# Four copies of an expert's first half, chosen by a jump per expert

## The chip, the cores and the metric

The kernel runs on one core of one Trainium2 chip. The metric is the device time of one execution in microseconds (us). Before the change it is 5404.11 us, the median of three runs from 5396.59 to 5407.47 us. Smaller is better.

A core has engines that run side by side, each with its own queue of instructions that it works through in order: TensorE (PE, matrix products and transposes), VectorE (DVE), ScalarE (ACT), GpSimd (POOL) and SyncE (SP, which here only starts transfers). They wait for each other by semaphores. A tile framework writes the waits; it also plans the order of each engine's queue by simulated times, and it may move an instruction ahead of others of the same straight stretch of code where its inputs are ready.

## The reference

One decoder layer in float32 on 8 sequences of 512 tokens of width 512 (N = 4096 tokens): a state-space block, a cross attention, and a mixture of experts, each followed by a layer norm. The change lies in the mixture of experts, and this is its core:

```python
E, K, CAP_FACTOR = 32, 4, 1.25
cap = max(1, int(CAP_FACTOR * N * K / E))          # 640 slots for each expert
w, idx = _gate(xf, wg)                             # 4 experts and weights for each token
oh = jax.nn.one_hot(idx.reshape(-1), E, dtype=jnp.int32)
pos = (jnp.cumsum(oh, axis=0) * oh).sum(-1) - 1    # place in the expert's queue
keep = pos < cap                                   # later tokens are dropped
...
xe = xp[buf_tok].reshape(E, cap, DIM)              # an empty slot holds zeros
h = silu(einsum('ecd,edh->ech', xe, w1)) * einsum('ecd,edh->ech', xe, w3)
out = einsum('ech,ehd->ecd', h, w2) * buf_w.reshape(E, cap, 1)
y = zeros((N + 1, DIM)).at[buf_tok].add(out)[:N]
z = silu(xf @ sw1) * (xf @ sw3) @ sw2              # the shared expert
return y + z
```

Every expert has 640 slots. How many of them hold a token depends on the data; 4096 x 4 / 32 = 512 is the mean. The slots are filled from the first on.

## The kernel before

`layers` does the first two blocks, the gate and the shared expert. For each token and chosen expert it computes a slot (`locate`; `taken[:, j, :]` counts the tokens of each expert so far, and after the last sequence `taken[:, SC, :]` holds the total of each expert) and scatters the token's row, with its weights and its own number behind it, into `xbuf` in DRAM (`send`). Slots that no token takes keep a row of zeros with the number of a spare row. `based` in DRAM holds the input of the last norm, to which the experts' outputs are added.

`experts` is the stage of the change. An expert has 640 slots, as five tiles of 128 (CJ = 5). For each expert e:

- `load(e)` starts four transfers on SyncE's queue: `xe` (640 rows, 1.36 MB, L1250) and the weights `w1`, `w3`, `w2` (1 MB each, L1253). Each has two buffers, so that one for expert e + 2 waits until expert e has finished with its own. For `xe` the last user is the last scatter of expert e, which reads the row numbers in it.
- `flip(j)` turns slot tile j by four transposes on TensorE (L1285) and an eviction on VectorE (L1286) into `xT`, with the model width on the partitions and the slots along the free dimension.
- `hidden(r)`, for r = 0 and 1, is the first half: `silu(x w1) * (x w3)`, written to `hT`. Each product is done by a scheme of seven block products in the place of eight (Strassen's, in Winograd's form): both operands are split in two by two blocks, and VectorE prepares sums of blocks (`sums_w`, L1276; `sums_x`, L1293 to L1296; `sums_w2`, L1308). The slots are split into two halves of HALF = 320 columns, slots 0 to 319 and 320 to 639. A block product is two matmul calls (L1314), each of which shows as two instructions in the profile; 2 x 2 x 7 x 2 x 2 = 112 instructions of 320 columns for each expert. ScalarE copies partial results out of PSUM (L1328) and applies silu (L1341), VectorE adds and multiplies (L1335, L1339).
- `give` is the second half: `hT w2`, seven block products for slots 0 to 511 (56 instructions of 256 columns), and a plain product for the fifth slot tile, slots 512 to 639 (L1416: four matmul calls, eight instructions of 512 columns). Outputs are scaled by the slot's weight (L1387, L1391, L1417, L1444), and `put(j)` on GpSimd's queue (L1394) adds the 128 rows of a slot tile to `based` by an indirect DMA that accumulates. The framework orders two `put`s, since both write `based`. The program's order of them is 4, 0, 1, 2, 3.

While `give` runs, a generator (`between`) puts the five `flip`s of the next expert between the products, and spreads `sums_x` and the sums of `w3` among them; the sums of `w1` of the next expert and of this one's `w2` go between the products of `hidden`. All 32 experts are written out one after the other, without a branch, so that the planner may also move work across experts.

## Time and profile before

| what | us |
|---|---|
| median of three runs | 5404.11 |
| the profiled execution's own time | 5406.28 |
| its span, first to last instruction | 5404.6 |
| TensorE busy in the span | 4672.4 (86%) |
| VectorE busy in the span | 4235.9 (78%) |
| expert stage, from the first transpose to the end of the last second half | 3794 to 5334 |
| in 3794 to 5334: TensorE busy | 1536.97 of 1540 |
| in 3794 to 5334: VectorE busy | 897.23 of 1540 |
| in 3794 to 5334: ScalarE busy | 426.77 of 1540 |

How to read it: a group row names the line, engine, operation, the tiles as written<-read, their shapes and how often (x); then busy time, the mean of one in ns, and idle time before it with what ended the idle time. A timeline row gives start, duration, engine, line and operation; the ends of matmuls are modelled, so that the distance from start to start is the rate. A windows row gives, for each stretch, its length, busy time of PE, PEld (weight loads), DVE, ACT and POOL with the number of instructions, the TensorE clock that was granted (1.00 is full), the share of the DMA engines' time and GB/s. `SPq` and `POOLq` are queues of those engines; a row of waits names who waited for what, for how long in all, how often, and the longest.

### The profile page before, as it was taken

How to read it: one execution, taken by the hardware profiler on the slowest of the kernel's cores; microseconds unless marked ns; L12 is line 12 of the kernel's file. 1: busy time of each engine (PE TensorE's matmuls, PEld its weight loads, DVE VectorE, ACT ScalarE, POOL GpSimd, SP SyncE). 2: the span in 40 equal slices, each digit the busy share in tenths (PEclk: the TensorE clock that was granted, in tenths of full speed). 3: DMA queues.
4: the chain of work that ended last, by engine and by line, in shares of the span. 5: the costliest groups of instructions: out<-in, count | busy, mean ns of one | idle time of the engine just before them, and what ended most of it. 6: DMA issues, size and time to landing. Idle time of an engine off the chain costs nothing. (4 is left out here: it accounts for less than half of the span.)

```text
span 5404.6 us, 53991 instructions
## 1 busy us (share of the span) xinstructions
PE 4672.4 (86%) x17320; PEld 2476.6 (46%) x17320; DVE 4235.9 (78%) x5369; ACT 2593.6 (48%) x5726; POOL 570.3 (11%) x426
## 2 busy tenths in 40 slices
PE   6768889788888988988888888789999999999994
PEld 3324234234333423433333342333677777777773
DVE  7999899989989989898998998943566555665554
ACT  5566565565656556566565655523222222222223
POOL 1000002002000200200200020011111111111111
PEclk8879989999999999999999999899999999999997
DMA  8875346345444634634544463342344444544544
GB/s 236 266 224 146 87 96 208 81 114 176 114 104 117 197 77 109 189 98 107 174 125 100 117 200 78 91 146 66 103 128 127 123 117 118 127 127 121 129 115 144
DMA packets 486427, 719.03 MB, mean 133 GB/s; under 512 B 117137, under 2 KB 200625, under 8 KB 484096
## 3 DMA queue, kind: packets, MB, share of 16 engines
q1 hardware_dynamic: 450128, 627.16, 41.1%
q0 software_dynamic: 33280, 76.90, 7.5%
q10 hardware_dynamic: 2736, 11.54, 0.5%
q8 instruction: 137, 2.24, 0.2%
q14 instruction: 146, 1.20, 0.1%
HBM read 391.24 MB, written 165.05 MB: 103 GB/s over the span
## 5 line engine op out<-in xcount | busy, mean ns | idle before, releaser
L480 ACT ACTIVATE l_da<-rep,l_aneg 128x256 f32<-128x256 f32 x2048 | 895.0, 501 | 941.8 <-DVE h L501 877.0
L501 DVE TENSOR_TENSOR_SCAN h<-l_da,h 128x1028 f32<-128x1028 f32 x512 | 1166.0, 2292 | 20.3 <-ACT l_da L480 17.7
L494 DVE TENSOR_TENSOR h<-rep,bc 128x1024 f32<-128x1024 f32 x512 | 614.7, 1218 | 103.1 <-PE py L521 84.6
L510 DVE TENSOR_TENSOR h<-h,bc 128x1024 f32<-128x1024 f32 x512 | 619.5, 1217 | 2.1
L521 PE MATMUL py<-h,l_fold 128*32 128x512 f32 x2048 | 368.3, 644 | 113.4 <-DVE h L510 96.5
L813 PE MATMUL ps_s<-l_ka,l_qa 64*128 64x512 f32 x1024 | 325.6, 707 | 137.8 <-DVE mx L815 137.6
L1314 PE MATMUL ps_h<-xT,w 128*128 128x320 f32 x1536 | 435.8, 433 | 0.0
L1394 POOL DMA_INDIRECT based<-y,xe x160 | 255.5, 1597 | 1309.9 <-ACT y L1417 630.0
L1335 DVE TENSOR_TENSOR hT<-ps_h,p 128x320 f32<-128x320 f32 x128 | 62.9, 492 | 378.5 <-PE ps_h L1314 378.5
L815 DVE TENSOR_REDUCE mx<-ps_s 128x2 f32<-128x1024 f32 x256 | 310.2, 1217 | 58.5 <-PE ps_s L813 58.3
L1314 PEld LDWEIGHTS ps_h<-xT,w 128*128 128x128 f32 x1536 | 292.5, 191 | 118.3 <-issue 0.4
L855 PE MATMUL po<-eT,l_va 128*64 128x512 f32 x1024 | 301.5, 670 | 47.6 <-ACT eT L843 43.1
L839 PE MATMUL ps_t<-l_qa,l_ka 64*128 64x512 f32 x1024 | 308.4, 674 | 23.8 <-ACT eT L843 23.1
L843 ACT ACTIVATE eT<-ps_t 128x1024 f32<-128x1024 f32 x256 | 259.0, 1015 | 128.8 <-PE ps_t L839 128.5
L688 POOL DMA_INDIRECT xbuf<-x2t,dest x128 | 217.2, 1697 | 860.4 <-DVE dest L679 760.8
L1314 PE MATMUL ps_h<-t,s 128*128 128x320 f32 x1024 | 286.1, 432 | 0.0
L343 PE MATMUL ps_z<-xnT,wm 128*128 128x256 f32 x1024 | 238.0, 388 | 30.0 <-DVE o L561 24.3
L750 PE MATMUL ps_p<-x2T,wa 128*128 128x512 f32 x512 | 241.5, 626 | 18.1 <-ACT hT L944 10.4
L552 PE MATMUL po<-wm,zs 128*128 128x512 f32 x512 | 244.7, 632 | 13.8 <-DVE z L957 11.9
L343 PE MATMUL ps_x<-xnT,wm 128*128 128x256 f32 x1024 | 246.5, 393 | 4.5 <-ACT xnT L332 2.5
L343 PEld LDWEIGHTS ps_z<-xnT,wm 128*128 128x128 f32 x1024 | 194.6, 193 | 93.0 <-DVE o L561 37.5
L343 PEld LDWEIGHTS ps_x<-xnT,wm 128*128 128x128 f32 x1024 | 196.1, 195 | 80.5 <-issue 43.8
(232 smaller groups left out, 7170.4 us busy)
## 6 DMA issues: line engine op xcount, KB each, us to landing
w<-in_w SPq DMA_DIRECT2D x93, 1024.0 KB
wm<-in_in_proj_w SPq DMA_DIRECT2D x128, 512.0 KB
rep<-dt SPq DMA_DIRECT2D x256, 256.0 KB
rep<-dtx SPq DMA_DIRECT2D x256, 256.0 KB
xbuf<-zero SPq DMA_DIRECT2D x32, 1362.5 KB
xe<-xbuf SPq DMA_DIRECT2D x32, 1362.5 KB
wm<-in_out_proj_w SPq DMA_DIRECT2D x64, 512.0 KB
wa<-in_sw SPq DMA_DIRECT2D x24, 1024.0 KB
```

The lines of the kernel that those rows point to most:

```text
L343: nc.tensor.matmul(ps[:, i, :], w[:, dc, i * P : (i + 1) * P], f["xnT"][:, dc, :], start=(dc == 0), stop=(dc == DC - 1),)
L480: nc.scalar.activation(da[:, n, 1:], dt[:, j, i, :], AF.Exp, scale=aneg[:, 2 * q + i, 2 * jj + j, g : g + 1])
L494: nc.vector.tensor_tensor(h[:, :, 1:], dtx.rearrange("p j i t -> p (j i) t"), f["bc", g][0], ALU.mult)
L501: nc.vector.tensor_tensor_scan(flat, da.rearrange("p n t -> p (n t)"), flat, 0.0, ALU.mult, ALU.add)
L510: nc.vector.tensor_tensor(h[:, :, 0:T], h[:, :, 1:], f["bc", g][1], ALU.mult)
L521: nc.tensor.matmul(f["py"][j * QP : (j + 1) * QP, :, :], fold, hs[j // 2][:, 2 * (j % 2) : 2 * (j % 2) + 2, 0:T], start=False, stop=g == N ...
L813: nc.tensor.matmul(ps[:, j, :], qa[r, lt * P : (lt + 1) * P], ka[r, :], start=True, stop=True)
L815: return lambda: nc.vector.tensor_reduce(mx[:, lt, :].unsqueeze(2), ps, AX.X, ALU.max) and None
L839: nc.tensor.matmul(ps[:, j, :], ka[r, kc * P : (kc + 1) * P], qa[r, :], start=True, stop=True)
L843: nc.scalar.activation(eT, ps, AF.Exp)
L855: nc.tensor.matmul(po[j * 2 * HD : (j + 1) * 2 * HD, :], va[:, kc, i, j * HD : (j + 2) * HD], eT[:, j, :], start=(kc == 0), stop=(kc == SC ...
L1314: nc.tensor.matmul(ps, w[:, n, r * P : (r + 1) * P], x[:, n, :], start=not more and n == 0, stop=n == 1, skip_group_check=more,)
```

## The change

The number of slots that an expert has to compute is chosen at run time from four: 448, 512, 576 and 640, that is 224, 256, 288 or 320 columns of each half.

- After the last sequence's `locate`, three VectorE instructions compute for each expert how many of the limits 448, 512 and 576 its count passes: `arm`, 0 to 3, kept in SBUF in a pool of its own.
- The two halves of the slots are now the even and the odd slots, so that the first `cols` columns of both halves hold slots 0 to 2 cols - 1. `flip` sorts them while it evicts, and `hidden` writes `hT` back in the order of the slots, with a stride of two.
- In the loop over experts, `tc.Switch` with four copies stands around the first half. TensorE, ScalarE and VectorE each read `arm` of the expert into a register, jump to one of the four copies, and jump out to common code after it; GpSimd and SyncE have nothing in the copies. The planner orders the inside of each copy by itself and moves nothing across the jumps.
- A copy zeroes the rest of `hT` where it has fewer than 320 columns, does `hidden` with `cols` columns, then the first two `flip`s of the next expert, and then the fifth slot tile (`fifth`): its product and its eviction where 2 cols > 512, and zeros in its output otherwise. `put(4)` is issued in all cases.
- The other three `flip`s stay in `give`. What the copies write is allocated ahead of them (`room_w`, `room_w2`, `got["y"]`, `nxt["xT"]`).
- For expert e + 1, each of the three engines loads the register in `give` of expert e and gives a hint of the coming jump (`announce`): VectorE behind the sums of `hT`, ScalarE behind the second copy `p1`, TensorE behind the products of the second block. Expert 0 has no hint.
- The PSUM pool of `flip` has two buffers in the place of one, the one of the fifth slot tile one in the place of two.

```diff
+COLS = tuple(range(224, HALF + 1, 32))
...
+        if not clock:
+            many = taken[:, SC, :]
+            more = taken[:, 1, :]
+            nc.vector.tensor_scalar(more, many, float(2 * COLS[0]), None, ALU.is_gt)
+            for c in COLS[1:-1]:
+                to = arm if c == COLS[-2] else more
+                nc.vector.scalar_tensor_tensor(to, many, float(2 * c), more, ALU.is_gt, ALU.add)
...
-    pst = ctx.enter_context(tc.tile_pool(name="e_pst", bufs=1, space=PSUM))
-    pso = ctx.enter_context(tc.tile_pool(name="e_pso", bufs=2, space=PSUM))
+    pst = ctx.enter_context(tc.tile_pool(name="e_pst", bufs=2, space=PSUM))
+    pso = ctx.enter_context(tc.tile_pool(name="e_pso", bufs=1, space=PSUM))
...
     def flip(got, j):
...
-        nc.vector.tensor_copy(got["xT"][:, :, j * P : (j + 1) * P], ps.rearrange("p (c t) -> p c t", c=DC))
+        to = got["xT"].rearrange("p c (k t) -> p c k t", k=2)[:, :, :, j * P // 2 : (j + 1) * P // 2]
+        nc.vector.tensor_copy(to, ps.rearrange("p (c t k) -> p c k t", c=DC, k=2))
...
     def product(ps, w, r, x, more=False):
 
+        cols = ps.shape[-1]
         for n in range(2):
-            nc.tensor.matmul(
-                ps, w[:, n, r * P : (r + 1) * P], x[:, n, :], start=not more and n == 0, stop=n == 1,
+            ins = nc.tensor.matmul(
+                ps, w[:, n, r * P : (r + 1) * P], x[:, n, 0:cols], start=not more and n == 0, stop=n == 1,
                 skip_group_check=more,
             )
-
-    def hidden(got, r, side):
+        return ins
+
+    def hidden(got, r, side, cols):
...
-            to = hT[:, 2 * i + r, k * HALF : (k + 1) * HALF]
+            to = hT.rearrange("p c (t k) -> p c t k", k=2)[:, 2 * i + r, 0:cols, k]
...
-    def give(e, got, side):
+    def fifth(e, got, cols):
+
+        j, y = CJ - 1, got["y"][CJ - 1]
+        if 2 * cols <= j * P:
+            nc.vector.memset(y, 0.0)
+            return
+        po = pso.tile([P, D], F32, tag="po", name="po")
+        for ic in range(DC):
+            nc.tensor.matmul(
+                po, got["hT"][:, ic, j * P : (j + 1) * P], got["w2"][:, ic, :], start=(ic == 0), stop=(ic == DC - 1)
+            )
+        nc.scalar.activation(y, po, AF.Identity, scale=got["x"][:, j, D + e : D + e + 1])
+
+    def give(e, got, side, which):
...
             v = p2.tile([P, HALF], F32, tag=f"{tag}{r}", name=tag)[:, 0:FH]
-            nc.scalar.activation(v, ps, AF.Identity, scale=weight(j))
+            ins = nc.scalar.activation(v, ps, AF.Identity, scale=weight(j))
+            if tag == "p1" and r and e + 1 < E:
+                announce(which, e + 1, ins)
             return v
...
-        for _ in sums_w(got, "hT"):
+        room_w(got, "hT")
+        for ins in sums_w(got, "hT"):
             pass
+        if e + 1 < E:
+            announce(which, e + 1, ins)
...
-        j = CJ - 1
-        po = pso.tile([P, D], F32, tag="po", name="po")
-        for ic in range(DC):
-            nc.tensor.matmul(po, hT[:, ic, j * P : (j + 1) * P], w2[:, ic, :], start=(ic == 0), stop=(ic == DC - 1))
-        nc.scalar.activation(ys[j], po, AF.Identity, scale=weight(j))
-        put(j)
+        put(CJ - 1)
...
+        if e + 1 < E:
+            announce(which, e + 1, ins)
...
     def between(nxt):
 
+        room_w(nxt, "w3")
         sums = sums_w(nxt, "w3")
-        for j in range(CJ):
+        for j in range(2, CJ):
             flip(nxt, j)
             if j == CJ - 1:
                 sums_x(nxt)
             next(sums, None)
             yield
+        for _ in sums:
+            pass
+
+    engines = {mybir.EngineType.PE: nc.tensor, mybir.EngineType.Activation: nc.scalar, mybir.EngineType.DVE: nc.vector}
+
+    def choice(k, e):
+        return engines[k].value_load(arm[0:1, e : e + 1])
+
+    def announce(which, e, ins):
+        k = ins.ins.engine
+        with tc.issue_after(ins.ins):
+            which[k] = choice(k, e)
+            tc.switch_hint({k: which[k]}, len(COLS), label=f"cols{e}")
...
+    which = {k: choice(k, 0) for k in engines}
     for e in range(E):
         got, nxt = nxt, load(e + 1) if e + 1 < E else None
         got["hT"] = p2.tile([P, DC, CAP], F32, tag="hT", name="hT", bufs=1)
-        for r in range(2):
-            hidden(got, r, sums_w2(got) if r == 0 else sums_w(nxt, "w1") if nxt else iter(()))
-        give(e, got, between(nxt) if nxt else iter(()))
+        room_w2(got)
+        got["y"] = [p2.tile([P, D], F32, tag="y", name="y", bufs=CJ + 2) for j in range(CJ)]
+        if nxt:
+            nxt["xT"] = p2.tile([P, DC, CAP], F32, tag="xT", name="xT")
+            room_w(nxt, "w1")
+        for n in tc.Switch(which, len(COLS), hint=f"cols{e}" if e else None):
+            if COLS[n] < HALF:
+                nc.vector.memset(got["hT"][:, :, 2 * COLS[n] :], 0.0)
+            for r in range(2):
+                side = sums_w2(got) if r == 0 else sums_w(nxt, "w1") if nxt else iter(())
+                hidden(got, r, side, COLS[n])
+            if nxt:
+                for j in range(2):
+                    flip(nxt, j)
+            fifth(e, got, COLS[n])
+        give(e, got, between(nxt) if nxt else iter(()), which)
```

More of the change, by code (lines that the diff above doesn't have):

```diff
@@ L86, in layernorm, with layers @@
     return wait(roots)
-def layers(ctx, tc, a, x1d, filld, based, xbuf):
+def layers(ctx, tc, a, x1d, filld, based, xbuf, arm):
     nc = tc.nc
@@ L1217, in layers, with experts @@
     dry()
-def experts(ctx, tc, a, xbuf, based):
+def experts(ctx, tc, a, xbuf, based, arm):
     nc = tc.nc
@@ L1263, in B, with room_w @@
         return x[:, 2 * j : 2 * j + 2, k * HALF : (k + 1) * HALF]
+    def room_w(got, n):
+        s1, s2, s4 = (wp.tile([P, 2, FH], F32, tag=f"{n}s{i}", name="s", bufs=1 if n == "hT" else 2) for i in (1, 2, 4))
+        got[n, "s"] = s1, s2, A(got[n], 1, 0), s4
     def sums_w(got, n):
         w = got[n]
-        s1, s2, s4 = (wp.tile([P, 2, FH], F32, tag=f"{n}s{i}", name="s", bufs=1 if n == "hT" else 2) for i in (1, 2, 4))
-        got[n, "s"] = s1, s2, A(w, 1, 0), s4
+        s1, s2, _, s4 = got[n, "s"]
         for o, x, y, op in (
@@ L1275, in sums_w @@
         ):
-            nc.vector.tensor_tensor(o, x, y, op)
-            yield
+            yield nc.vector.tensor_tensor(o, x, y, op)
     def flip(got, j):
-        if j == 0:
-            got["xT"] = p2.tile([P, DC, CAP], F32, tag="xT", name="xT")
         ps = pst.tile([P, D], F32, tag="tr", name="ps_t")
@@ L1296, in sums_x, with room_w2 @@
         nc.vector.tensor_tensor(t4, B(x, 1, 0), t2, ALU.subtract)
+    def room_w2(got):
+        got["t2"] = [wp.tile([P, 2, FH], F32, tag=f"w2t{i}", name="t", bufs=1) for i in range(4)]
     def sums_w2(got):
         w = got["w2"]
-        got["t2"] = t1, t2, t3, t4 = [wp.tile([P, 2, FH], F32, tag=f"w2t{i}", name="t", bufs=1) for i in range(4)]
+        t1, t2, t3, t4 = got["t2"]
         for o, x, y in (
@@ L1326, in keep @@
         def keep(ps, m, tag):
-            v = p2.tile([P, HALF], F32, tag=f"{tag}{m}", name=tag)
+            v = p2.tile([P, HALF], F32, tag=f"{tag}{m}", name=tag)[:, 0:cols]
             nc.scalar.copy(v, ps)
@@ L1345, in hidden @@
         for m, (w, s1, s2, s3, s4) in enumerate(ws):
-            xs[m] = psx.tile([P, HALF], F32, tag="h", name="ps_h")
+            xs[m] = psx.tile([P, HALF], F32, tag="h", name="ps_h")[:, 0:cols]
             product(xs[m], A(w, 0, 0), r, B(x, 0, 0))
@@ L1349, in hidden @@
         for m, (w, s1, s2, s3, s4) in enumerate(ws):
-            ps = psy.tile([P, HALF], F32, tag="h2", name="ps_h")
+            ps = psy.tile([P, HALF], F32, tag="h2", name="ps_h")[:, 0:cols]
             product(ps, A(w, 0, 1), r, B(x, 1, 0))
@@ L1359, in hidden @@
         for m, (w, s1, s2, s3, s4) in enumerate(ws):
-            ys.append(psy.tile([P, HALF], F32, tag="h2", name="ps_h"))
+            ys.append(psy.tile([P, HALF], F32, tag="h2", name="ps_h")[:, 0:cols])
             product(ys[m], s1, r, t1)
@@ L1379, in give @@
         both = range(2)
-        ys = [p2.tile([P, D], F32, tag="y", name="y", bufs=CJ + 2) for j in range(CJ)]
+        ys = got["y"]
         def weight(j):
@@ L1421, in give @@
             ps = psy.tile([P, HALF], F32, tag="h2", name="ps_o")[:, 0:FH]
-            product(ps, A(hT, 0, 1), r, BW(w2, 1, 0))
+            ins = product(ps, A(hT, 0, 1), r, BW(w2, 1, 0))
             use(r, 0, ps, p1[r])
+        if e + 1 < E:
+            announce(which, e + 1, ins)
         for r in both:
@@ L1461, in experts @@
     for n in ("w1", "w3"):
+        room_w(nxt, n)
         for _ in sums_w(nxt, n):
             pass
+    which = {k: choice(k, 0) for k in engines}
     for e in range(E):
@@ L1466, in experts @@
         got["hT"] = p2.tile([P, DC, CAP], F32, tag="hT", name="hT", bufs=1)
-        for r in range(2):
-            hidden(got, r, sums_w2(got) if r == 0 else sums_w(nxt, "w1") if nxt else iter(()))
-        give(e, got, between(nxt) if nxt else iter(()))
+        room_w2(got)
+        got["y"] = [p2.tile([P, D], F32, tag="y", name="y", bufs=CJ + 2) for j in range(CJ)]
+        if nxt:
+            nxt["xT"] = p2.tile([P, DC, CAP], F32, tag="xT", name="xT")
+            room_w(nxt, "w1")
[10 more added lines that the diff above has]
+        give(e, got, between(nxt) if nxt else iter(()), which)
 def finish(ctx, tc, based, out):
@@ L1518, in program @@
     nc = tc.nc
-    with tc.tile_pool(name="dram", bufs=1, space=DRAM) as dram:
+    with tc.tile_pool(name="dram", bufs=1, space=DRAM) as dram, tc.tile_pool(name="one", bufs=1) as one:
         x1d = dram.tile([N, D], F32, name="x1d")
@@ L1524, in program @@
         xbuf = dram.tile([SLOTS, ROW], F32, name="xbuf")
+        arm = one.tile([P, E], I32, name="arm")
         nc.scalar.preload_act_table_set(LN_EXP)
         with ExitStack() as ctx:
-            layers(ctx, tc, a, x1d, filld, based, xbuf)
+            layers(ctx, tc, a, x1d, filld, based, xbuf, arm)
         with ExitStack() as ctx:
-            experts(ctx, tc, a, xbuf, based)
+            experts(ctx, tc, a, xbuf, based, arm)
         with ExitStack() as ctx:
```

## The prediction

> **What bounds the kernel now.** First the page: over the whole span TensorE is busiest, and its row of slices stands at 9 for the last quarter, the expert stage. There I read TensorE's timeline over one expert, e = 10 (its first half ends and its second half begins at 4312.36).

> ```profile
> PE 4672.4 (86%) x17320; PEld 2476.6 (46%) x17320; DVE 4235.9 (78%) x5369; ACT 2593.6 (48%) x5726; POOL 570.3 (11%) x426
> PE   6768889788888988988888888789999999999994
> ```
> ```profile
> 4312.36 0.60 PE L1285 MATMUL ps_t<-e_ident,xe 128*128 128x128 f32 x4
> 4312.79 1.89 PE L1314 MATMUL ps_o<-w,hT 128*128 128x256 f32 x8
> 4314.52 3.60 PE L1416 MATMUL po<-w,hT 128*128 128x512 f32 x8
> 4317.96 0.60 PE L1285 MATMUL ps_t<-e_ident,xe 128*128 128x128 f32 x4
> ...
> 4330.43 4.47 PE L1314 MATMUL ps_h<-xT,w 128*128 128x320 f32 x16
> 4334.74 4.47 PE L1314 MATMUL ps_h<-t,s 128*128 128x320 f32 x16
> ...
> 4360.58 0.60 PE L1285 MATMUL ps_t<-e_ident,xe 128*128 128x128 f32 x4
> ```

> Columns: start, duration, engine. From start to start nothing is idle: sixteen 320-column instructions take 4334.74 - 4330.43 = 4.31 us, 269 ns each; eight of 256 take 1.73 (216 ns); eight of 512 take 3.44 (430 ns); four transposes 0.43. All are 0.84 ns a column, down to 128, so columns removed are time removed. One expert takes 48.2 us: first half 112 x 0.269 = 30.1, second half 56 x 0.216 + 3.44 + 5 x 0.43 = 17.7.

> Next, what follows close behind. The reading `xe` of the next expert is on SyncE's queue behind the scatters of the expert before (two `xe` buffers); the POOL and SP timelines and the waits of SP show it:

> ```profile
> 4328.82 1.54 POOL L1394 DMA_INDIRECT based<-y,xe  x1 [8.16 <-DVE y L1391]
> 4335.53 1.56 POOL L1394 DMA_INDIRECT based<-y,xe  x1 [5.16 <-DVE p L1335]
> 4341.16 1.55 POOL L1394 DMA_INDIRECT based<-y,xe  x1 [4.07 <-DMA based<-y,xe]
> 4347.10 1.54 POOL L1394 DMA_INDIRECT based<-y,xe  x1 [4.39 <-issue]
> ```
> ```profile
> 4351.97 0.37 SPq L1250 DMA_DIRECT2D xe<-xbuf  x1
> ```
> ```profile
> SPq L1250 <- DMA based<-y,xe: 696.7, 71, 24.0
> ```
> ```profile
> 4351.90:4357.90 6.00, 6.00 (x24) 4.19 (x23) 1.75 (x4) 1.75 (x4) 0.00 (x0) 1.00 0.72 233
> 4357.90:4360.50 2.60, 2.60 (x11) 1.84 (x10) 1.12 (x3) 0.91 (x2) 0.00 (x0) 1.00 0.00 0
> ```

> The last row pair (windows; the last three columns are clock, DMA share, GB/s) shows the transfer end at 4357.9. The second half of e = 10 ended at 4330.6. The four scatters add into one tensor, so each waits for the one before, some 5.6 us apart; the last lands 21.4 us after the half's end, then `xe` needs 5.9. So **xe is in 27.3 us after a second half ends, whatever TensorE does**, and today's first transpose comes 30.1 us after it. The slack is 2.7 us.

> **The change, part by part.** The reference, evaluated on its own inputs, sends to the 32 experts: at most 448 tokens 12 times, 449 to 512 5 times, 513 to 576 6 times, more 9 times. So 12 experts run the 224-column copy, 5 the 256, 6 the 288, 9 the 320.

> *Columns and fifth tile removed.* A first half becomes 112 x 0.84 ns x columns: 21.1, 24.1, 27.1 or 30.1 us. Gain 12 x 9.0 + 5 x 6.0 + 6 x 3.0 = 156. The fifth tile's 3.44 goes in 17 experts: 58. Together -215 on TensorE; taken alone, 5191.

> *Two transposes moved* to the end of the first half, before the jump out. They need the next `xe`, hence not before 27.3 us. TensorE queues in order: the fifth tile and the whole second half stand behind them. The wait is 27.3 - 21.1 = 6.2 us in 12 experts, 3.2 in four (the last expert has no next), 0.2 in six: **+88**. A second half ending sooner does not help: the scatters count from its end.

> *The clock after such a wait.* Windows on two pauses of TensorE in earlier stages (the column after POOL's count is the granted clock):

> ```profile
> 3459.80:3464.40 4.60, 0.00 (x0) 0.00 (x0) 4.60 (x6) 2.79 (x10) 0.00 (x0) 0.83 0.74 129
> 3464.40:3469.70 5.30, 5.26 (x8) 1.68 (x9) 2.93 (x4) 0.20 (x1) 0.00 (x0) 0.50 0.94 199
> 3469.70:3475.00 5.30, 5.30 (x14) 2.36 (x13) 5.30 (x8) 1.71 (x4) 0.00 (x0) 1.00 0.59 144
> ```

> After 4.6 us without a matmul the clock was 0.50 for 5.3 us of work, a loss of 2.6; after a pause of 8.1 (2590 to 2598) it was 0.50 for 4.6 us, 2.3. I take 2.4 for each of the 12 long waits and 1.7 (one 3.4 us stretch, as after the 3.2 us pause at 3322) for the four: **+36**, between 0 and 45.

> [...]

> *The jump out.* TensorE's next product reads `hT`, written on VectorE, which must first pass the end of its copy, behind the two transposes' evictions (L1286, 0.69 each); with the fifth tile, behind ScalarE's 0.69 eviction instead. Nearest rows: one eviction plus a handover, 1.0 (`xT` at 4313.03 ends 1.35 after its first transpose started); none if the wait names the earlier instruction. I take 0.7 x 31 = **+22**, ends 0 and 53 (1.7).

> *VectorE in the second half.* In 4312.4 to 4330.4 it is busy 16.05 of 18.0 us. Without the fifth tile TensorE needs 56 x 0.216 + 3 x 0.43 = 13.4; VectorE still has 4 + 4 sums (0.69), 4 sums of `xT` (0.82), 3 copies and 6 evictions (0.44): 13.5, starting a microsecond late, with its register load among them. It holds up PSUM buffers and the first scatter by about 0.8 us in 17 experts: **+14**, ends 0 and 51. The next waiter is `xe`, which counts from that scatter.

> *Register loads, hints, jumps.* Three engines, each expert: a load of the count, a hint, a jump in, a jump out. No row shows any of them. Below: nothing, since TensorE has products of 216 ns queued while its sequencer reads; a gain is excluded. Above: waiting for code. The instruction queue q8 moved 137 packets of 16 KB in 0.2% of 16 engines' time, 0.2% x 16 x 5404.6 / 137 = 1.3 us each; two jumps, 2.6 an expert, 83 in all. The hints stand some 10 us ahead of their jump and the exit's a whole half ahead, nearer the lower end: 0.5 x 32 = **+16**.

> [...]

> *At nothing:* zero fills of `hT` and tile 5 on VectorE (the first half keeps it busy 12.1 of 30.2 us; even in 21 us there is room; without that cover about 1.5 us each for 23 experts); the strided writes of `hT`, same cover (if each of its 20 operations took half as long again, 5 us, still inside); three gate operations, 0.17 each, once; PSUM buffers swapped between transposes and the fifth tile (the transposes wait 2.6 us in all for L1286 today). Loads on SP keep their order of release; sums of the weights that VectorE now does a whole expert early (it even waits 1.6 us for `w` at 4317.8) return to their own expert, `w1` in the first half.

> **Sum:** -215 + 88 + 36 + 22 + 14 + 16 = -39. The profiled execution took 5406.28 us (span 5404.6), 2 above the median of 5404.11. So 5367 for it, **5365** beside the median.

> **The rivals.** 0.2% (11 us) is about what a measurement of this kernel tells from none.
> 1. *Slower: the jumps wait for their code.* Without the jump term the sum is -55, so above 55 / 32 = 1.7 us an expert the change loses. At 1.95, the longest of the 16 KB packets in this stage (they run from 0.88), on 32 exits and on the 16 entries that no `xe` wait covers, 48 x 1.95 = 94: 5443. For it: nothing in the trace has ever jumped. Against: the hints' lead over packets of about 1 us.
> 2. *The waits cost less:* clock kept, handovers hidden: 5404 - 215 + 88 + 16 = 5293. Against: the pauses in the windows.
> 3. *`xe` does not hold,* -215 + 22 + 14 + 16: 5241. Against: 71 waits of SP on scatters, and only 2.7 us slack.
> 4. *No fewer columns:* all experts full, only overheads, +38. The counts exclude it unless the choice is wrong.

> **How the numbers follow.** Forecast 0.45 (5340 to 5393), second rival 0.12, third 0.03: faster 0.60. Half-hidden jumps, within 11 us: 0.09. Slower 0.31, nearly all the first rival. The range runs from the second rival, 5290, to a little past the first, 5450. The forecast's own, for signs are mixed: 5340 to 5393.

> **What would show it.** TensorE idle before L1285's transposes, ended by `xe`, about 6 us in 12 experts and 3 in four; granted clock below 1.00 in the stage (now 1.00); 17320 - 17 x 8 = 17184 matmuls; 320-copy experts at 48 to 50 us, 224-copy at about 46; the scatters still 5.6 us apart. Wrong if idle time sits after the jumps with no releaser, if `xe` lands earlier, or if the planner puts the transposes elsewhere.

## The result, and the profile after

The kernel with the jumps takes 5460.2 us (median of four runs, 5449.7 to 5466.5), the kernel before, run beside it on the same chip, 5405.8 (5396.6 to 5408.3). The ratio is 1.0102, 95% interval 1.0079 to 1.0124: **slower by 1.0%**, where 0.7% faster was forecast. The time lies 10 us above the upper end of the range.

The page of the profiled execution after, rows that answer to those shown of before:

```profile
span 5448.0 us, 55096 instructions
PE 4531.9 (83%) x17184; PEld 2469.3 (45%) x17184; DVE 4204.0 (77%) x5412; ACT 2549.7 (47%) x5709; POOL 569.6 (10%) x426
PE   6768889888888888978888888788978789898984
q8 instruction: 211, 3.46, 0.3%
q14 instruction: 336, 2.75, 0.1%
```

TensorE runs 17184 matmuls, as forecast, and is 140 us less busy; but its last quarter, a row of nines before, now shows sevens and eights. The last two rows are the queues of kind `instruction`, which I read as those that bring code: 211 packets of 16 KB and 336 of 8 KB, where before it was 137 and 146. So the work went, and more than its time came back as idle time in the expert stage. Who waited there, by the view of waits for 3800 to 5380 us (total us, times, longest):

```profile
DVE s L1288 <- issue: 107.5, 23, 6.1
PE ps_t L1294 <- DMA xe<-xbuf: 71.5, 15, 8.9
PE ps_o L1328 <- DVE y L1421: 28.2, 35, 0.9
PE ps_o L1328 <- DVE s L1288: 27.0, 16, 3.6
PE ps_h L1328 <- DVE hT L1350: 21.0, 24, 2.6
PE ps_h L1328 <- ACT p L1343: 13.3, 10, 2.8
DVE t L1321 <- issue: 25.7, 8, 4.5
ACT p L1343 <- issue: 20.2, 4, 5.4
PE ps_h L1328 <- issue: 10.4, 2, 5.7
PE ps_t L1294 <- issue: 10.3, 6, 2.0
```

"issue" means that the engine waited for nothing that the profile shows. The first row is VectorE at its first work behind the copies (the sums of `hT`), 23 times, 4.7 us each: just the 23 experts that did not run the last copy. TensorE waits for `xe` 15 times, and then for what VectorE and ScalarE bring late: `s` and `y` in the second half, `hT` and `p` in the first. Its own two rows of "issue" are two ways into a copy and six ways out. One expert, e = 24 (224 columns), by the timelines of TensorE and of VectorE:

```profile
5016.79 0.35 PE L1328 MATMUL ps_h<-t,w 128*128 128x224 f32 x1
5023.66 3.05 PE L1294 MATMUL ps_t<-e_ident,xe 128*128 128x128 f32 x12 [6.52 <-DMA xe<-xbuf]
5026.51 2.70 PE L1328 MATMUL ps_o<-w,hT 128*128 128x256 f32 x8
...
5032.52 1.97 PE L1328 MATMUL ps_o<-t,s 128*128 128x256 f32 x8 [1.14 <-DVE s L1288]
...
5035.82 2.12 PE L1328 MATMUL ps_o<-t,s 128*128 128x256 f32 x8 [0.90 <-DVE y L1421]
...
5042.20 1.99 PE L1328 MATMUL ps_o<-t,hT 128*128 128x256 f32 x8 [0.80 <-DVE y L1421]
```
```profile
5025.64 0.69 DVE L1296 COPY xT<-ps_t 128x512 f32<-128x512 f32 x1 [0.16 <-PE ps_t L1294]
5030.96 0.69 DVE L1288 TENSOR_TENSOR s<-hT 128x512 f32<-128x512 f32 x1 [4.62 <-issue]
```

The first half ends at 5017.1, 6.5 us of waiting for `xe` follow, and the second half takes from 5026.5 to 5044.0, 17.5 us, where its 56 products and three flips need 13.4; 2.8 us of the difference are the three waits shown. VectorE's last work in the copy ends at 5026.3; its next instruction runs at 4.6 us after that. In the trace's own instruction records the jump out of the copy ends at 5025.7, and a packet of 8 KB of queue q14 lies at 5029.2, inside the gap: I read this as VectorE waiting for code, and the experiments test it. Windows over the same stretch (the third column from the right is the granted clock, then the DMA share):

```profile
5017.50:5023.60 6.10, 0.00 (x0) 0.00 (x0) 0.14 (x1) 0.00 (x0) 1.42 (x1) 0.81 0.95 272
5023.60:5028.00 4.40, 4.32 (x16) 3.71 (x17) 1.38 (x2) 0.00 (x0) 0.00 (x0) 0.50 1.06 352
5028.00:5032.50 4.50, 3.38 (x17) 2.62 (x17) 1.51 (x3) 0.95 (x2) 0.00 (x0) 0.98 0.35 130
```

After the wait the clock is 0.50 for 4.4 us; behind the pauses of 4.6 and 8.1 us in the trace of before it was 0.50 for 5.3 and 4.6 us.

What a jump costs, from the instruction records of the whole stage (end of the jump to the first instruction that is behind it; for the way out, the first instruction in common code; copies are numbered by their place in the program). TensorE's next instruction follows within 0.15 us of its jump; its wait lies in the record of the jump itself, mostly 0.3 to 0.4 us where it does not wait:

| engine, way | copy next in line | other copies |
|---|---|---|
| VectorE in | copy 0: 0.46 us (once 4.3) | 4.0 to 4.2 (twice 0.48) |
| VectorE out | copy 3: 0.74 | 5.3 to 6.3 |
| ScalarE in | copy 0: 0.36 | 2.5 to 5.5, mostly 3.2 |
| ScalarE out | copy 3: 0.38 | 2.3 to 5.1 |
| TensorE in (idle) | copy 0: none, but 4.6 and 5.7 in two of 12 | none (3.8 at expert 0, which has no hint) |
| TensorE out (idle) | copy 3: none, but 1.9 once | copies 0 and 1: none; copy 2: 1.4 to 2.0 in five of six |

(Medians of a copy, or the range.) Copy 0 lies right behind the jump and copy 3 right ahead of the common code. VectorE and ScalarE, which the prediction had not looked at, wait for nearly whatever is not next in line. TensorE's jump out of copy 2 takes 3.9 to 5.5 us and once, out of copy 3, 5.4; the fifth tile's products, queued ahead of it, cover the most of that. The prediction's sign of being wrong, idle time behind the jumps with no releaser, is there. Experts with 224 columns take 43.9 to 50.6 us, 48.0 in the mean, where about 46 was said; those with 320 take 50.1 to 57.0, where 48 to 50 was said.

The instruction records also show 63 hints on each of the three engines: the 31 that `announce` gives, 8 to 18 us ahead of the jump in, and 32 that stand at the head of the copies, at the line of `tc.Switch`, 20 us and more ahead of the jump out.

### The profile page after: what moved, and what is told of

Same layout as the page of the kernel before. It is cut to its first block, busy times and chain, and to the rows that moved or that the text cites. A ratio compares the mean times of both kernels' runs of the same rounds, so it can differ in the third digit from the quotient of the medians.

```text
span 5448.0 us, 55096 instructions
## 1 busy us (share of the span) xinstructions
PE 4531.9 (83%) x17184; PEld 2469.3 (45%) x17184; DVE 4204.0 (77%) x5412; ACT 2549.7 (47%) x5709; POOL 569.6 (10%) x426
## 3 DMA queue, kind: packets, MB, share of 16 engines
q1 hardware_dynamic: 450128, 627.16, 40.5%
## 4 chain that ended last, share of the span: by engine, by line
DVE 37%; PE 23%; DMA 16%; issue 16%; ACT 6%; SPq 2%; DVEq 0%; POOL 0%; POOLq 0%; ACTq 0%
DVE h L502 14%; DMA based<-y,xe 9%; PE ps_h L1328 6%; DVE h L495 5%; DVE h L511 5%; PE ps_p L758 3%; PE po L553 3%; DVE mx L823 2%; DVE xs L378 2%; PE ps_s L821 2%; ACT l_da L481 2%; PE ps_t L847 2%; PE po L863 2%; PE ps_o L1328 1%; PE py L522 1%
## 5 line engine op out<-in xcount | busy, mean ns | idle before, releaser
L1328 PE MATMUL ps_h<-xT,w 128*128 128x224 f32 (+3 forms) x1536 | 375.2, 395 | 14.2 <-issue 10.4
L847 PE MATMUL ps_t<-l_qa,l_ka 64*128 64x512 f32 x1024 | 304.6, 666 | 24.1 <-ACT eT L851 23.3
L1328 PE MATMUL ps_h<-t,s 128*128 128x224 f32 (+3 forms) x1024 | 253.1, 396 | 34.5 <-DVE hT L1350 21.0
L553 PE MATMUL po<-wm,zs 128*128 128x512 f32 x512 | 246.6, 637 | 13.4 <-DVE z L965 11.7
L758 PE MATMUL ps_p<-x2T,wa 128*128 128x512 f32 x512 | 242.3, 628 | 18.0 <-ACT hT L952 10.4
L1350 DVE TENSOR_TENSOR hT<-ps_h,p 128x224 f32<-128x224 f32 (+3 forms) x128 | 55.8, 436 | 260.5 <-PE ps_h L1328 259.5
```

The costliest lines, as they stand in the source:

```text
L553: nc.tensor.matmul(pos[j], yg[:, c, j * P : (j + 1) * P], w[:, i, :], start=(c == 0), stop=(c == CC - 1))
L847: nc.tensor.matmul(ps[:, j, :], ka[r, kc * P : (kc + 1) * P], qa[r, :], start=True, stop=True)
L1328: ins = nc.tensor.matmul(ps, w[:, n, r * P : (r + 1) * P], x[:, n, 0:cols], start=not more and n == 0, stop=n == 1, skip_group_check=more,)
```

## The experiments

Two theories stood at first. **Theory 1**: the jumps of VectorE and ScalarE wait for code, and TensorE waits for them. **Theory 2**: what the change rearranged (even and odd slots, fifth tile early, transposes ahead of the join) or the waits for `xe` took the gain. Ratios below are to the kernel before, run beside each on the same chip (medians 5402.4 to 5405.7). Line numbers shift by up to six between kernels, so go by the tiles: `s` at 1282 or 1283 is 1288 above, `ps_o` and `ps_h` at 1322 or 1323 are 1328, `t<-w` at 1316 is 1321, `y<-ps_o` at 1415 is 1421, `ps_t` at 1288 or 1289 is 1294, `p<-ps_h` at 1338 is 1343, `po` at 1393 is 1398.

### The rearrangement without jumps

```diff
-        for n in tc.Switch(which, len(COLS), hint=f"cols{e}" if e else None):
+        for n in (len(COLS) - 1,):
```

Register loads, hints and the gate's operations go as well. All experts have 320 columns.

> No jump, no register load, no choice: each expert's first half is the 320-column copy, written out once, and the planner is free again across experts. All else of the change stays (even and odd slots, strided hT, two transposes and the fifth tile at the end of the first half, PSUM buffers). Theory 1 (the jumps cost, because VectorE and ScalarE wait for code): 5400 to 5415, as before the change. Theory 2 (the new order of the work costs, jumps or not): 5425 or more.

Measured: 5400.4, ratio 0.9993 (0.9982 to 1.0003). The rearrangement costs nothing; Theory 2 loses that part.

### The narrow experts without jumps

The same, with `for n in (ARMS[e],)`, where ARMS holds the numbers that these inputs give. The choice at run time is left out.

> No jump: the width of each expert's first half is fixed beforehand from this input's counts (12 x 224, 5 x 256, 6 x 288, 9 x 320), so the work of the chosen copies is done in straight-line code. Theory 1 with the wait for xe as predicted (88) and the half clock behind it (36): 5404 - 215 + 88 + 36 = 5313, 5300 to 5335. If xe holds nobody: 5190 to 5230. Theory 2 (order, VectorE in the second half): 5350 or more.

Measured: 5348.3, ratio 0.9897 (0.9881 to 0.9914). Straight code gets 55 of the 215 us that the removed work is worth; the jumps cost the rest of the way, 5460.2 - 5348.3 = 112 us, 3.5 an expert. The wait for `xe` explains most of what is missing here, by the waits of 3800 to 5330:

```profile
PE ps_t L1288 <- DMA xe<-xbuf: 124.3, 22, 9.2
```

22 waits of 5.7 us, where the prediction had 12 of 6.2, four of 3.2 and six of 0.2, 88 us in all: the transposes that wait for `xe` start 27.8 to 30.3 us after a second half, not 27.3, and without jumps TensorE has no other wait of any size.

### Without hints, and with late ones

```diff
-            tc.switch_hint({k: which[k]}, len(COLS), label=f"cols{e}")
```

> The changed kernel without the hints; register loads and jumps stay. In the trace ScalarE needs 0.36 us to enter the first copy, which lies right behind the jump, and 2.5 to 5.5 us for any other, and leaves the last copy in 0.38 us and the others in 2.3 to 5.1: by this the hints do nothing there, and the time is 5450 to 5475. If the hints help TensorE, whose 32 entries mostly show no wait, its entries into the three other copies (20) would cost 3 to 5 us more: 5500 to 5560.

Measured: 5529.0, ratio 1.0227 (1.0209 to 1.0245), 69 us more than with hints. (The 32 hints at the heads of the copies stay.) TensorE's way in, by the waits of the stage:

```profile
PE ps_h L1328 <- issue: 88.4, 19, 5.6
```

With hints it was 10.4 us in two waits (shown above), both at copy 0, where TensorE never waits without hints. So hints do work for TensorE, for the copies that are not next in line. In the instruction records VectorE's way in is 5.5 us without a hint and 4.2 with, ScalarE's 4.1 and 3.2: for these two a hint takes about a microsecond off. Is theirs too early? VectorE's register load and hint go from the start of the second half to behind its last eviction, ScalarE's from its second copy `p1` to its second `p5`; TensorE's stay.

```diff
-            if tag == "p1" and r and e + 1 < E:
+            if tag == "p5" and r and e + 1 < E:
                 announce(which, e + 1, ins)
...
-            nc.vector.scalar_tensor_tensor(ys[j][:, k * FH : (k + 1) * FH], ps, weight(j), more, ALU.mult, ALU.add)
+            ins = nc.vector.scalar_tensor_tensor(ys[j][:, k * FH : (k + 1) * FH], ps, weight(j), more, ALU.mult, ALU.add)
+            if j == 3 and k == 1 and e + 1 < E:
+                announce(which, e + 1, ins)
```

> The changed kernel with VectorE's and ScalarE's register load and hint moved from the start of the second half to its end (VectorE: behind the last eviction that uses slot tile 3; ScalarE: behind the last of the four evictions before the end), 2 to 6 us ahead of the jump instead of 11 to 13; TensorE's stays. If the hinted code is there but is overwritten before the jump: VectorE's way in falls from 4.2 us to about 0.5, ScalarE's from 3.2 to 0.4, some 2 to 3 us for each of the 20 experts outside copy 0: 5395 to 5430 against 5460. If hints do little for these two engines wherever they stand: 5450 to 5475. If the fetch needs its lead: towards the kernel without hints, 5475 to 5530.

Measured: 5459.0, ratio 1.0103 (1.0086 to 1.0120): the same as the changed kernel. By the instruction records VectorE's hint now stands 0.4 to 1.5 us ahead of its jump (before: 8 to 16) and ScalarE's 4.7 to 5.8 (before: 10 to 18), not the 2 to 6 and 11 to 13 of the expectation. VectorE's way in stays at 4.2 to 4.4 us, ScalarE's becomes 3.5 to 4.2. Later hints bring nothing; why a hint serves TensorE and hardly the other two was not found out.

### Four equal copies, always the last or always the first

```diff
-COLS = tuple(range(224, HALF + 1, 32))
+COLS = (HALF,) * 4
...
+            nc.vector.memset(arm, 3)
```

(0 in the place of 3 for the first copy.) Nothing is saved, so that the time is the price of jumping.

> Four identical copies of 320 columns, and the number in `arm` is set to 3 for every expert: nothing is saved, every jump leads to the last copy, which lies right ahead of the join. Theory 1 (VectorE and ScalarE wait about 4.2 and 3.2 us for the code of a copy that is not next in line, and leave the last one for nothing): the copies of 320 columns took 50.1 to 52.9 us in the changed kernel against 47.9 before, 2.2 to 5.0 us each, so 31 x 3 = 93 us over the kernel before: 5465 to 5520. Rival 2 (the price is register reads, hints and the restart of VectorE after the join, the same for every copy, 0.5 to 1.3 us): 5410 to 5440, and the same as with copy 0.

> The same with `arm` set to 0: every jump leads to the first copy, which lies right behind the jump, and the way out is a jump over the three others. Theory 1: entry costs 0.4 us on VectorE and ScalarE, the way out 5.3 us on VectorE; TensorE has two transposes and the fifth tile's eight products (some 5 us) between the first half and the first product that needs VectorE's sums, so most of the 5.3 us is covered: 0.5 to 2 us per expert, 5420 to 5465, and less than with the last copy. Rival 2: the same as with the last copy, 5410 to 5440.

Measured: last copy 5532.0, ratio 1.0245 (1.0224 to 1.0266); first copy 5524.2, ratio 1.0232 (1.0212 to 1.0251). That is 130 and 122 us, 4.1 and 3.8 an expert. My numbers for Theory 1 were too small for both, and that the two are alike is what Rival 2 said; but at three times its price and more, and in different places. Last copy, VectorE, ScalarE and TensorE at one entry (timelines; the second half before it is undisturbed):

```profile
4426.05 1.29 DVE L1316 TENSOR_TENSOR t<-w 128x512 f32<-128x512 f32 x2 [4.44 <-issue]
```
```profile
4428.55 0.75 ACT L1338 COPY p<-ps_h 128x320 f32<-128x320 f32 x2 [5.22 <-issue]
```
```profile
4422.65 4.47 PE L1323 MATMUL ps_h<-xT,w 128*128 128x320 f32 x16
4429.02 4.81 PE L1323 MATMUL ps_h<-t,s 128*128 128x320 f32 x16 [1.90 <-ACT p L1338]
```

First copy, VectorE and TensorE at one exit:

```profile
4409.87 0.69 DVE L1283 TENSOR_TENSOR s<-hT 128x512 f32<-128x512 f32 x1 [5.10 <-issue]
```
```profile
4403.68 3.60 PE L1393 MATMUL po<-w,hT 128*128 128x512 f32 x8
4410.58 0.66 PE L1289 MATMUL ps_t<-e_ident,xe 128*128 128x128 f32 x4 [3.29 <-DVE s L1283]
```

and TensorE's waits at those transposes in the whole stage (3800 to 5480):

```profile
PE ps_t L1289 <- issue: 49.6, 18, 3.4
PE ps_t L1289 <- DVE s L1283: 25.8, 8, 3.7
```

With the last copy TensorE starts the first half at once and stands 1.9 us later, when its PSUM buffers are full and ScalarE has not come. With the first copy the first half is untouched (30.1 us of products) and TensorE stands 3.3 us behind the fifth tile. The view names VectorE's `s` in 8 of 26 such waits, but these transposes do not read `s`. In the instruction records TensorE's own jump out lasts from 4403.62 to 4410.52 here, and in all 26 its first transpose starts 0.06 us after the end of its own jump, which takes 5.9 to 7.3 us; VectorE's sums have begun 0.7 us before that in the example. So TensorE stands at its own jump, in spite of the hint at the head of the copy; VectorE, 5.9 us late behind its jump, might have held it nearly as long, which this run does not separate. The fifth tile's 3.4 us cover only a part of either. Theory 1 stands in that the jumps wait, with a larger size; but TensorE's own jump has to be counted with those of VectorE and ScalarE.

### Taking away the wait for the rows

Three buffers for `xe` in the kernel with jumps:

```diff
-        got["x"] = xe = p2.tile([P, CJ, ROW], F32, tag="xe", name="xe")
+        got["x"] = xe = p2.tile([P, CJ, ROW], F32, tag="xe", name="xe", bufs=3)
```

> The changed kernel with three buffers for xe instead of two, so that xe of the next expert is there a whole expert earlier. The trace of the changed kernel has TensorE idle for 71.5 us on xe, and some 30 us of lost clock behind it. If these cost what they show: 5360. If the time sits in the jumps of VectorE and ScalarE and only changes its name when xe comes early: 5390 to 5450. If xe costs nothing: 5460.

Measured: 5410.4, ratio 1.0011 (1.0001 to 1.0021). The waits for `xe` are gone; VectorE's wait at the way out stays (100.5 us in 23), and two others grow: VectorE waits 58.3 us for weights in `s`, and TensorE 63.8 us for `y`. Is that the jumps alone? The same in straight code:

> The straight-line kernel with 224 to 320 columns by the known counts (no jump), with three buffers for `xe`. Theory 1 with the row wait: in the version with two buffers (5348) the waits for `xe` and the half clock after them were all that kept it from the sum of removed work (5404 - 215 = 5190): now 5190 to 5240. Rival 3 (short first halves are also bound by the weights' transfers or by ScalarE and VectorE, which do the same number of instructions): 5270 to 5340.

Measured: 5277.5, ratio 0.9767 (0.9748 to 0.9785). Rival 3's number: 88 us above the 5190 of the removed work were left without any jump. The waits (3800 to 5400) name weights:

```profile
DVE s L1282 <- DMA w<-in_w: 77.4, 22, 7.5
PE ps_o L1322 <- DVE y L1415: 64.6, 20, 7.4
```

Three runs tried to bring the weights forward on SyncE's queue and did not.

```diff
-        nc.sync.dma_start(xe, xbuf[e * CAP : (e + 1) * CAP, :].rearrange("(j p) d -> p j d", p=P))
-        for n in ("w1", "w3", "w2"):
+        for n in ("w1", "w3"):
             got[n] = w = wp.tile([P, DC, D], F32, tag=n, name=n)
             start(w, a[n][e].rearrange("(c p) f -> p c f", p=P))
+        nc.sync.dma_start(xe, xbuf[e * CAP : (e + 1) * CAP, :].rearrange("(j p) d -> p j d", p=P))
...
```

> The changed kernel with three buffers for `xe`, as the run that took 5410, but with the transfers of the next expert's `w1` and `w3` put ahead of that of `xe` in SyncE's queue. There VectorE waited 58 us for weights that stood behind an `xe` that waits for scatters, and TensorE 64 us for VectorE's outputs. If the order in the queue is the cause: 5345 to 5380. Rival (the wait is for something else, so that the order changes nothing): 5400 to 5415.

Measured: 5417.8, ratio 1.0024 (1.0013 to 1.0035). In the trace the queue still issues `xe` first and `w1`, `w3` half a microsecond or more behind it; the planner has kept its own order. This run therefore tells nothing about the order. Four buffers:

> The straight-line kernel with 224 to 320 columns by the known counts, with four buffers for `xe`. With three (5277) VectorE waited 77 us for weights whose transfers stood on SyncE's queue behind an `xe` that waits for scatters, and TensorE some 65 us for VectorE's outputs. Theory: with a fourth buffer `xe` waits for scatters that are long done, the weights start earlier, and the time nears the sum of the removed work: 5190 to 5230. Rival (the 16 DMA engines cannot bring the weights faster than a short expert uses them): 5260 to 5285.

> The changed kernel (jumps, four copies) with four buffers for `xe`. With three it took 5410, with 58 us of VectorE waiting for weights and 64 us of TensorE waiting for VectorE's outputs. If the queue behind `xe` is the cause: 5340 to 5375, that is 125 us or so, the price of the jumps as the two runs with four equal copies gave it (5524 and 5532 against 5402), above the straight-line version with four buffers. Rival (short experts are bound by VectorE's way out of the copy alone): 5400 to 5415.

Measured: 5273.2, ratio 0.9754 (0.9738 to 0.9770), and 5414.8, ratio 1.0022 (1.0012 to 1.0032), both as with three. With one more buffer the planner issues `xe` one expert further ahead, and it waits for the same scatters as before, with the weights behind it. So `xe` went to another queue, GpSimd's, which issues the scatters anyway:

```diff
-        nc.sync.dma_start(xe, xbuf[e * CAP : (e + 1) * CAP, :].rearrange("(j p) d -> p j d", p=P))
+        (nc.gpsimd if e > 1 else nc.sync).dma_start(xe, xbuf[e * CAP : (e + 1) * CAP, :].rearrange("(j p) d -> p j d", p=P))
```

> The straight-line kernel with 224 to 320 columns by the known counts and three buffers for `xe`, with `xe` issued from GpSimd's queue from expert 2 on, so that no weight stands behind an `xe` that waits for scatters. On SyncE's queue it took 5277 (5273 with four buffers). If the order in the queue causes VectorE's 60 to 77 us of waiting for weights and TensorE's 50 to 65 us for VectorE's outputs: 5195 to 5240. Rival (the transfers themselves are too slow for a short expert, or the wait is for something else): 5255 to 5285.

> The changed kernel (four copies, jumps) with three buffers for `xe` and `xe` on GpSimd's queue. With SyncE's it took 5410, with 58 us of VectorE waiting for weights. If the order in the queue is the cause: 40 to 75 us less, 5335 to 5370. Rival: 5400 to 5420.

Measured: straight 5205.6, ratio 0.9643 (0.9626 to 0.9660); with jumps 5393.6, ratio 0.9982 (0.9971 to 0.9993). In straight code the same two rows are now

```profile
DVE s L1282 <- DMA w<-in_w: 14.4, 14, 1.8
PE ps_o L1322 <- DVE y L1415: 7.1, 11, 0.9
```

and the expert stage stands at clock 1.00 with TensorE busy 1312.75 of 1320 us. Taking `xe` out of that queue brought 72 of the 88 us: 199 of the nominal 215 us are there. (Which transfer VectorE's sums of `w3` wait for the trace does not tell; their own weights had been issued an expert earlier.) The same step brings the kernel with jumps 17 us, not the 40 to 75 I expected: with nothing else to wait for, the jumps cost 5393.6 - 5205.6 = 188 us, 5.9 an expert. That is more than the 112 of the kernels with two buffers, so that there a part of the jumps' time lay beside the wait for `xe`.

### Why one jump takes so long

ScalarE's way out in the changed kernel falls in two groups. Worked out from the instruction and packet records, with the share of the 16 DMA engines' time that was busy in the 3 us after the jump:

```
DMA share 0.08 to 0.81 (16 experts): 2.34 to 2.92 us
DMA share 1.00 or more  (7 experts):  4.55 to 5.10 us
```

(Six of the seven are the six ways out of copy 2, so that the copy could be the cause as well.) And VectorE's way out took 2.8 us at experts 30 and 31, where no weights are left to load. The page counts the packets of q8 and q14 (0.3% and 0.1% of the 16 DMA engines' time) on the same engines as the weights' (q1, 40.5%), and `w1` and `w3` start just when a first half ends (5017.3 in the expert shown). Test: the kernel with four equal copies, first copy, without later weight transfers.

```diff
+    kept = {}
     def load(e):
...
+            if e > 1:
+                got[n] = kept[n, e % 2]
+                continue
-            got[n] = w = wp.tile([P, DC, D], F32, tag=n, name=n)
+            kept[n, e] = got[n] = w = wp.tile([P, DC, D], F32, tag=n, name=n)
```

> The kernel with four equal copies of 320 columns, always the first (5524), with the weights of experts 0 and 1 used again by all later experts: 90 transfers of 1 MB are left out, and the output is that of other weights. VectorE's way out took 5.9 us there with weights under way and 2.7 us at the last expert with idle DMA engines; its excess over the cover was 3.4 us per expert. If the code's own transfer waits behind the weights': 2.7 to 3 us everywhere, 30 x 3.1 = 93 us less, 5415 to 5445. Rival (the wait has nothing to do with the weights): 5510 to 5530.

Measured: 5424.0, ratio 1.0036 (1.0024 to 1.0047), 100 us less than with the weights. VectorE's waits for code behind the copy, with weights, then without:

```profile
DVE s L1283 <- issue: 152.5, 32, 5.2
```
```profile
DVE s L1288 <- issue: 64.4, 32, 2.6
```

VectorE's way out falls from 5.9 to 2.8 us (medians), and TensorE's jump out from 5.9 to 7.3 us in 26 experts to 0.4 in 31 of 32. In VectorE's way out the packets of q14 show where the time lies: without weights the first begins 0.9 to 1.2 us after the jump, with them 3.5 to 4.2 (in 29 of the first 30 experts), and it takes 0.3 to 0.6 us in both. So the code waits ahead of its own transfer. Of the 122 us that jumping to the first copy costs, 100 are there only while weights are loaded: TensorE's idle time in the stage falls by 77 us, 75 of them the two rows of `ps_t` above, and its busy time by 21, as the clock is 0.98 in the mean with weights and 1.00 without.

### Three attempts at a better version

Two copies (256 and 320), with four buffers for `xe`, then with `xe` on GpSimd's queue:

```diff
-COLS = tuple(range(224, HALF + 1, 32))
+COLS = (256, HALF)
```

> Two copies, 256 and 320 columns, and four buffers for `xe`. 17 experts are in the first copy: 17 x (6.0 + 3.4) = 160 us of products less, 5403 - 160 = 5243. Jumps: out of the first copy some 5.5 us of waiting for VectorE with no fifth tile to cover it, 17 x 5.5 = 94; into the second 2.3 us in the first half and 1.2 after it, 14 x 3.5 = 49. Sum 5386: 5360 to 5400. If the second copy's place right ahead of the join makes no difference, as much as with four copies, 5400 to 5420.

> Two copies, 256 and 320 columns, three buffers for `xe` on GpSimd's queue. With four buffers on SyncE's queue it took 5397, with 34 us of VectorE waiting for weights and 30 us of TensorE waiting for VectorE's outputs. If the order in the queue is the cause: 15 to 35 us less, 5360 to 5382. Rival: 5390 to 5405.

Measured: 5396.6, ratio 0.9986 (0.9974 to 0.9998), and 5417.5, ratio 1.0034 (1.0022 to 1.0045). The first came close to its sum, the second missed it: on GpSimd's queue two copies are slower than four, and I did not find out why.

The sums of `hT` inside the copies, ahead of VectorE's way out, with two copies and four buffers (VectorE's register load and hint move behind its first eviction of the second half):

```diff
-        room_w(got, "hT")
-        for ins in sums_w(got, "hT"):
-            pass
...
+            for _ in sums_w(got, "hT"):
+                pass
             fifth(e, got, COLS[n])
```

> The same with the sums of `hT` moved from the second half into the copies, so that VectorE jumps out only after them and TensorE's first products of the second half need nothing from behind VectorE's jump. If VectorE's way out is what the first copy loses (17 x 5.5 us), part of it now lies beside TensorE's first 12 products of the second half: 2 to 4 us less for each of 17 experts, 5310 to 5355. Rival (TensorE then waits as long for the evictions that come next): within 10 us of the version without the move.

Measured: 5522.5, ratio 1.0210 (1.0193 to 1.0228), 126 us more than without the move. The waits are those that the rival named, at a larger size (without the move the first row was 30.5 us):

```profile
PE ps_o L1328 <- DVE y L1421: 114.6, 30, 7.5
DVE xT L1296 <- issue: 71.8, 15, 5.5
```

TensorE ran ahead only until its PSUM buffers were full (its 30 waits for `y`, 114.6 us); the evictions stand behind the jump, and behind the sums that now come ahead of it. VectorE's waits for weights grew too, from 34.0 to 96.0 us, so that the 126 us have more than one cause.

`xe` and all weights of expert e + 2 on GpSimd's queue behind the second scatter of expert e:

```diff
+        if e + 2 < E:
+            with tc.issue_after(last.ins):
+                return load(e + 2, True)
```

> The changed kernel (four copies) with three buffers for `xe`, and with `xe` and all three weights of expert e + 2 issued on GpSimd's queue behind the second slot tile's scatter of expert e (some 6 us after its second half has ended), where no engine jumps until the end of the next first half, some 15 us later. With `xe` alone on GpSimd's queue it took 5394. If the jumps wait for their code behind the weights: the 17 ways out of copies 0 and 1 and the 20 ways in some 2 and 1.3 us less each, 34 + 26 = 60: 5315 to 5350. Rival (the weights' transfers then hold the scatters, or the jumps wait as long): 5380 to 5410.

Measured: 5840.0, ratio 1.0803 (1.0785 to 1.0821).

```profile
PE ps_h L1328 <- DVE hT L1350: 487.7, 30, 17.5
DVE s L1288 <- DMA w<-in_w: 484.2, 30, 18.7
```

This was a mistake of mine in the reading of the order: the sums of the next expert's `w1` stand among the products of the current first half, so weights that are issued after the second half before it come some 16 us late, 30 times. It says nothing about the jumps. Of all versions that choose at run time, four copies with `xe` on GpSimd's queue is the fastest (5393.6, hardly to be told from the 5396.6 of two copies with four buffers), 0.2% below the kernel before, about the size that can be told from nothing.

## Why the prediction was wrong

The straight kernels take the sum apart:

| steps | predicted | measured | from |
|---|---|---|---|
| columns and fifth tile removed; VectorE in the second half | -215 + 14 | -199 | 5205.6 - 5405.1 (straight, `xe` on GpSimd's queue) |
| two transposes moved; the clock after such a wait | +88 + 36 | +143 | 5348.3 - 5205.6 |
| the jump out; register loads, hints, jumps | +22 + 16 | +112 | 5460.2 - 5348.3 |
| sum | -39 | +56 | 5460.2 - 5405.8 = +54 |

The measured column adds up by construction, since each run stands in two differences. It also depends on the order: with the wait for `xe` taken away first, the jumps cost 188 us, not 112, and taking it away in the kernel with jumps brought 67 us (5460.2 - 5393.6), not 143.

- *Columns and fifth tile removed*: right. 17184 matmuls, and in straight code all but 16 us of the 215. *VectorE in the second half* is in the same difference; of its 14 us the rows show 7.1, in 11 waits of TensorE for `y`.
- *Two transposes moved*: right in mechanism and place, too small. The waits for `xe` in straight code are 124 us where 88 stood; in the changed kernel, where the jumps take their share, 71.5. TensorE's transposes that waited started 27.4 to 30.8 us after a second half, where 27.3 was said, and the weights stand behind `xe` in the same queue (in the expert shown, SyncE starts `xe` at 5016.7 and `w1`, `w3` at 5017.3, at the end of the first half, so that the three are under way together; that this is what delays `xe` was not tested). Three buffers took away the waits for `xe` but not those for what stands behind it; the other queue did.
- *The clock after such a wait*: right; 0.50 for 4.4 us behind the wait shown (in the trace of before 0.50 for 3.4 us, 3326.3 to 3329.7, behind the 3.2 us pause), and, worked out from the clock records, some 39 us of TensorE's time in the expert stage of the straight kernel with two buffers, where 36 was said.
- *The jump out*, 22 us, was costed as evictions and a handover, and ***Register loads, hints, jumps***, 16 us, as two waits of at most a packet. **These are the terms that were mis-sized: together 112 where 38 stood, and they alone turn the sign.** Both had upper ends (53 and 83) that hold the 112, though not the 188; I took values near the lower ends because "the hints stand some 10 us ahead of their jump and the exit's a whole half ahead". Both leads are there in the trace, but they do not hide the wait: the entry's hint hides it for TensorE alone, and the exit's, 20 us and more ahead, for neither VectorE nor ScalarE, nor for TensorE out of copy 2. The upper end itself was drawn from packets: a packet's time is not the time of a wait for it. VectorE's packet took 0.3 to 0.6 us, and its wait was 2.7 to 3.0 us without weights and mostly 5.3 to 6.1 with them. Of the 112 us TensorE's idle time shows 69 (193 us in the changed kernel, 124 in the straight one); the rest I did not break down.
- *Rival 1* is what happened: its threshold of 1.7 us an expert was passed at 3.5. That its price (5443) lies near the measured 5460 is partly luck, for its place was mostly wrong: it counted 48 waits of TensorE at its own jumps. In the changed kernel those are 10.4 + 10.3 us; the larger waits are for what VectorE and ScalarE bring late behind theirs (`y`, `s`, `hT` and `p`, 89.5 us together).
- *The jumps of VectorE and ScalarE* took, but for three of their 128 in the changed kernel, 0.4 to 0.7 us to code that is next in line and 2.3 to 6.9 to other code. I gave too much weight to the lead of a hint, which no row had shown to work.
- *At nothing*: confirmed for the rearrangement as a whole, ratio 0.9993 with 320 columns and no jumps.

## What to carry to other kernels

Here a jump on an engine that feeds a saturated TensorE was, but for three jumps of 128, a wait of 2.3 to 6.9 us unless its target was the next code in line (0.4 to 0.7), and TensorE's own was one too where its hint did not serve (its jump out of copy 2 took 3.9 to 5.5 us). Count it for every engine that jumps, in and out, and ask what the DMA engines carry at that moment: without weight transfers VectorE's wait behind the first copy was half as long (2.8 us in place of 5.9). Before work is removed from the busiest engine, find what arrives close behind it, and what stands behind that in the same queue: here 215 us of work bought 55 until the rows went to a queue of their own, and then 199. Costs that lie beside a wait come out when the wait goes: the same jumps cost 112 us with the wait for `xe` and 188 without it.
